# Start-up loads put into their order of use, and two small matrix products folded into one with two column groups

## The chip, the core and the metric

The kernel runs on one core of a Trainium2 chip. The metric is the device time of one execution in microseconds (us); less is better. Everything is float32.

## The reference

The reference adds two blocks to an input `x` of 2 sequences with 1024 tokens of 256 features. The first block (an attention layer with a "field", then a mixture of 64 small experts) is the only one that the change touches, and there only its attention. Cut to what matters:

```python
qkv = x @ Wqkv.T + bqkv                        # 16 heads of 16
attn = softmax(q @ k.T / sqrt(16))
coh = sigmoid(tanh([x, cs] @ Wc1.T + bc1) @ Wc2.T + bc2)   # cs: one row of 64 per sequence
mod = attn * coh;  mod = mod / (mod.sum(-1) + 1e-8)
fp = layernorm(relu(cs @ We1.T + be1) @ We2.T + be2)       # one row of 256 per sequence
pe = sin(pos / inv)                            # a table, 1024 x 256
fa = softmax(fp @ pe.T)                        # 2 x 1024: the field
mod = (1 - FI) * mod + FI * fa[:, None, None, :]
out = (mod @ v) @ Wout.T + bout
```

The field `fa` is small: for each of the 2 sequences one softmax over 1024 positions.

## The kernel before

The engines are TensorE (PE), VectorE (DVE), ScalarE (ACT), GpSimd (POOL) and SyncE (SP). A framework sets the semaphores, and also the order of instructions on each engine, from a schedule that it works out when the program is built. Inside a `manual_schedule` block PE, DVE and ACT keep the order in which the code is written; POOL and SP do not, they get what the framework's schedule finds ready.

**Loads.** At the start, ACT issues the load of `cols` (L107), then three parts of the attention weights `w_att`: the first halves of `wq` and `wk` and the whole of `wv` (L155 to L165). SP issues the two halves of `xT` for sequence 0 (L134, L135), then the second halves of `wq` and `wk`, and `wout`. POOL issues `w_cs`, `w_pro`, `rows`, `xT` for sequence 1 and the table `peT` (L468 to L474).

**The lead (L680 to L717).** The attention works on 8 units of 16 steps. Each step of `maxima(step, half)` (L304) makes 2 x 2 score products into a two-bank PSUM tile `pm`, and DVE reduces each tile to its row maxima (L320). Such tiles come from `wide` (L180), which turns through three of them in this part: one of pool `ps_3`, two of `ps_s`. A step makes two tiles, so the second tile of step m+1 needs the buffer that the first tile of step m held only after DVE has read it. All the rest takes single PSUM banks from `one` (L195), two buffers in turn.

Ahead of the lead stand the q and k projections of unit 0 (`project_part`, L280), `spread(0)` (L297; eight SP transfers that scatter the heads into `km` and `qm`), `from_state`, two `coherence_in` (L535: two products, then a tanh on ACT), and two `values` (L204: products into `pv`, then, as here `lead` is set, an ACT copy into `v`, L224, and a POOL add of the bias, L225).

The lead itself is 12 steps; after the two `maxima` of step m come the pieces of `fill[m]`:

```python
[field_in, coherence_in(0, 1, 0)],           # m = 0
[field_mean, coherence_in(0, 1, 1)],
[field_var, values(0, 1, 0)],
[values(0, 1, 1), spread(1)],                # then matrices()
[field_logits(0)],  [field_logits(1)],       # m = 4, 5
[coherence_in(1, 0, 0), field_weights],  [coherence_in(1, 0, 1), field_scale],
[coherence_in(1, 1, 0)],  [coherence_in(1, 1, 1), field_out],
[shift(0), rotation(mats)],  [coherence_out]
```

`matrices` (L492) is called after step 3 and makes, on POOL, two 256 x 256 matrices out of 32 blocks of 64 x 64 (L506). `field_logits(n)` (L628) multiplies `fpc` (128 x 2) with half n of `peT` into a bank of 2 rows x 512 columns, takes the row maxima and their negative on DVE, and the exp and its sum on ACT. `field_weights` (L647) combines the halves' maxima on DVE (`fall`), makes weights on ACT (`fw`), and sums on POOL. `field_scale` (L654) takes a reciprocal on DVE, scales `fw` on POOL and the two halves of `fe` on ACT. `field_out` (L660) turns `fe` by eight transposes on PE into `fac`.

**Behind the lead.** 128 steps follow (L770), each with score products, exps, the product with `v` (L365) and, while there are any, the `maxima` of twelve steps later. `between` (L732 to L765) hangs other pieces on some of them; L756 hangs `values(1, n, part)` for both parts on step 2 and 5 of unit 2. Then come the experts and the second block, which the change does not touch.

## Time and profile before

| | us |
|---|---|
| median of 3 runs | 1551.67 (1550.71 to 1555.02) |
| the profiled execution's own time | 1551.6 |
| its span, first to last instruction | 1549.8 |
| PE / DVE / ACT / POOL busy | 1528.1 / 891.1 / 881.5 / 529.3 |
| first matmul starts | 6.44 |
| first score product of the 128 steps (L347) starts | 63.38 |

The profiled execution is 0.07 us under the median, and 1.8 us of it lie outside the span. The table is read as follows: PE is busy for 99% of the span, and the other engines for 34% to 57%. All that the change touches lies in the first 63.4 us of the span, except for one piece in unit 2, at 184 us. Times given as places ("at 48.21") are us from the span's start. A line of the trace's timeline gives the start, the length, the engine and line, the operation with what it writes and reads, how many instructions are merged into it, and in brackets the idle time of the engine before it.

### The profile page before, as it was taken

To read this page: it belongs to the slowest core of one execution; us is meant where nothing else is said; L and a number is where in the kernel's file an instruction comes from. 1 tells how busy PE (TensorE), PEld (TensorE's weight loads), DVE (VectorE), ACT (ScalarE), POOL (GpSimd) and SP (SyncE) were. 2 spreads that over 40 slices of the span, in tenths; PEclk is the share of its full clock that TensorE was granted. 3 is DMA by queue.
4 is the path that set the end of the run, shared out by engine and by line. 5 is a ranking of instruction groups with operands and counts; after the bars stand their busy time and mean duration, and the time that the engine had idled before them with its cause. 6 is when DMAs were issued, how large, how long until landed. Compare 5 with 4: busy or idle time off the path is not lost.

```text
span 1549.8 us, 25956 instructions
## 1 busy us (share of the span) xinstructions
PE 1528.1 (99%) x10176; PEld 754.1 (49%) x10176; DVE 891.1 (57%) x1606; ACT 881.5 (57%) x1710; POOL 529.3 (34%) x863
## 2 busy tenths in 40 slices
PE   8999999999999999999999999999999999999999
PEld 4333343333333444444687667555555454545544
DVE  5868768776873222224455766656666565656531
ACT  2478768787887222224334554665757666666641
POOL 3333323333430100000102354555555555565411
PEclk9999999999999999999999999999999999999999
DMA  5100000010000526445843202000100001000001
GB/s 165 56 14 15 1 15 15 1 21 8 1 1 15 172 96 194 150 144 180 265 163 96 65 5 84 1 1 1 68 2 2 14 1 57 1 18 12 23 6 41
DMA packets 50441, 84.90 MB, mean 55 GB/s; under 512 B 4616, under 2 KB 25392, under 8 KB 50064
## 3 DMA queue, kind: packets, MB, share of 16 engines
q1 hardware_dynamic: 47776, 77.41, 16.0%
q0 software_dynamic: 1584, 5.29, 1.1%
q8 instruction: 80, 1.31, 0.3%
q10 hardware_dynamic: 960, 0.56, 0.1%
q14 instruction: 41, 0.34, 0.1%
HBM read 57.02 MB, written 22.02 MB: 51 GB/s over the span
## 4 chain that ended last, share of the span: by engine, by line
PE 93%; DVE 3%; ACT 2%; DMA 2%; POOL 0%; issue 0%; SPq 0%; ACTq 0%; POOLq 0%; DVEq 0%
PE pga L1451 9%; PE sc L347 9%; PE po L365 8%; PE pm L313 7%; PE lg L816 7%; PE sl L842 7%; PE pq L1161 7%; PE cmb L935 6%; PE py L1485 4%; PE pwo L1382 4%; PE po L1362 3%; PE pv L1231 3%; PE sc L1274 2%; PE pqk L283 2%; PE py L863 2%; PE pe L1246 2%
## 5 line engine op out<-in xcount | busy, mean ns | idle before, releaser
L320 DVE TENSOR_REDUCE mx<-pm 128x2 f32<-128x1024 f32 x256 | 301.5, 1219 | 108.1 <-PE pm L313 108.0
L355 ACT ACTIVATE e<-sc 128x512 f32<-128x512 f32 (+1 forms) x500 | 263.6, 614 | 67.8 <-PE pm L313 63.6
L347 PE MATMUL sc<-qs,km 32*128 32x512 f32 x1024 | 247.8, 617 | 0.7 <-ACT cg L565 0.7
L313 PE MATMUL pm<-km,qm 32*128 32x512 f32 x1024 | 242.9, 616 | 0.0
L383 POOL TENSOR_TENSOR ob<-ob,part 128x512 f32<-128x512 f32 x101 | 128.4, 1271 | 251.2 <-ACT part L382 251.2
L1451 PE MATMUL pga<-hc,w 128*128 128x512 f32 x320 | 143.0, 598 | 2.0 <-ACT eT L1349 0.8
L365 PE MATMUL po<-e,v 128*32 128x512 f32 x1024 | 136.9, 605 | 0.0
L347 PEld LDWEIGHTS sc<-qs,km 32*128 32x128 f32 x1024 | 91.7, 183 | 86.5 <-ACT e L355 65.2
L1328 POOL TENSOR_SCALAR eall<-eall,den 128x192 f32<-128x192 f32 (+1 forms) x128 | 113.8, 902 | 26.8 <-DVE den L1324 26.8
L935 PE MATMUL cmb<-xb,y 128*128 128x256 f32 x512 | 117.4, 383 | 0.0
L1161 PE MATMUL pq<-wqo,xa 128*128 128x512 f32 x256 | 116.1, 597 | 0.1
L816 PE MATMUL lg<-phi,xa 128*128 128x512 f32 x256 | 116.1, 596 | 0.0
L1312 ACT ACTIVATE eall<-eall,nmx 128x192 f32<-128x192 f32 (+1 forms) x256 | 111.1, 439 | 8.0 <-DVE nmx L1295 7.8
L842 PE MATMUL sl<-dsp,xb 128*128 128x512 f32 x256 | 114.9, 593 | 0.0
L1199 POOL TENSOR_TENSOR t<-raw,tabs 128x512 f32<-128x512 f32 x64 | 80.7, 1283 | 96.7 <-ACT raw L1191 96.6
L313 PEld LDWEIGHTS pm<-km,qm 32*128 32x128 f32 x1024 | 83.4, 184 | 49.2 <-DVE mx L320 34.9
L826 DVE TENSOR_TENSOR l<-lg,keep 128x512 f32<-128x512 f32 x32 | 22.1, 692 | 144.8 <-ACT keep L824 144.8
L935 PEld LDWEIGHTS cmb<-xb,y 128*128 128x128 f32 x512 | 95.5, 190 | 17.7 <-issue 4.4
L1451 PEld LDWEIGHTS pga<-hc,w 128*128 128x128 f32 x320 | 59.5, 190 | 73.0 <-issue 68.0
L1295 DVE CUSTOM_DVE_ANT_0 eall<-sc,mask,zn 128x192 f32<-128x192 f32 (+1 forms) x256 | 86.9, 405 | 7.0 <-PE sc L1274 7.0
L824 ACT COPY keep<-lg 128x512 f32<-128x512 f32 x32 | 18.7, 584 | 126.0 <-issue 101.0
L1191 ACT COPY raw<-pq 128x1024 f32<-128x1024 f32 x32 | 32.4, 1011 | 97.6 <-PE pq L1161 97.6
(228 smaller groups left out, 2366.3 us busy)
## 6 DMA issues: line engine op xcount, KB each, us to landing
lgd<-keep SPq DMA_DIRECT2D x64, 256.0 KB, 2.4
w<-in_ffn_W SPq DMA_DIRECT2D x16, 1024.0 KB, 7.1
ebig<-lgd SPq DMA_DIRECT2D x64, 256.0 KB, 3.6
wqo<-in_wqkv SPq DMA_DIRECT2D x2, 1536.0 KB, 7.7
w<-in_w SPq DMA_DIRECT2D x2, 1386.0 KB, 5.9
km<-hk SPq DMA_DIRECT2D x32, 64.0 KB, 2.3
qm<-hq SPq DMA_DIRECT2D x32, 64.0 KB, 2.3
phi<-in_phi SPq DMA_DIRECT2D x1, 2048.0 KB, 7.5
```

Source lines behind the costliest of these rows:

```text
L313: nc.tensor.matmul(pm[:, x, :], qm[u % 2][r, i * P : (i + 1) * P], km[u % 3][r, n * 512 : (n + 1) * 512], start=True, stop=True,)
L320: nc.vector.tensor_reduce(mxs[hu][:, i % 4, 2 * half : 2 * half + 2, n], pm, AX.X, ALU.max)
L347: nc.tensor.matmul(sc[:, x, :] if both else sc[x], km[u % 3][r, j * P : (j + 1) * P], qs[u % 2][r, n * 512 : (n + 1) * 512], start=True, s ...
L355: nc.scalar.activation(part, t, AF.Exp, scale=1.0 / HD0**0.5)
L365: nc.tensor.matmul(po[32 * hh : 32 * hh + 32, :], v[b][:, j, at : at + 32], es[s, hh // 2][:, hh % 2, :], start=True, stop=True,)
L383: nc.gpsimd.tensor_tensor(obs[u, n], obs[u, n], part, ALU.add)
L816: nc.tensor.matmul(lg[:, b, :], xa[:, k, b, 1 + m * P : 1 + (m + 1) * P], phi[:, k, n * 512 : (n + 1) * 512], start=(k == 0), stop=(k == 1),)
L842: nc.tensor.matmul(accs[n][b][:, c, :], xo_tm[:, b * 8 + m, c * P : (c + 1) * P], d[:, b, :], start=(m == 0), stop=(m == 7),)
L935: nc.tensor.matmul(acs[q][:, c, :], y[b][:, 4 * jj + j, c * P : (c + 1) * P], eT[:, j // 2, j % 2 * 256 : (j % 2 + 1) * 256], start=(jj == ...
L1161: nc.tensor.matmul(pq[:, x, :], shifted(xa, k, b, w * WIN, P), load["wqkv"][:, k, x * 512 : (x + 1) * 512], start=(k == 0), stop=(k == 1),)
L1328: engine.tensor_scalar(e[:, x, c, lo:KEYS], e[:, x, c, lo:KEYS], den[:, x, c : c + 1], None, ALU.mult)
L1451: nc.tensor.matmul(pt[:, x, :], load["w1"][:, k, lo : lo + P], hcs[f][:, k, :], start=(k == 0), stop=(k == 1))
```

## The change

1. The start-up loads. ACT now issues only `cols` and the first halves of `wq` and `wk` ahead. SP issues, behind the two halves of `xT`, the loads `w_cs`, `w_pro`, `wv` and `rows`. POOL issues no load at all. Behind the second tanh, ACT issues five more: `peT`, `xT` of sequence 1, the second halves of `wq` and `wk`, and `wout`.
2. `field_logits` is called once. `fpc`, filled up with zeros to 32 columns (`fpz`), is the weight of two column groups of the array, one for each half of `peT`; the results lie in partitions 0 to 31 and 32 to 63 of one bank. Maximum, negative and exp are then one instruction each, on 64 partitions.
3. To combine the halves, `field_weights` first copies the maxima and sums of the two groups side by side, with four copies on POOL; the DVE minimum (`fall`) now reads what those copies wrote. `field_scale` copies the weights back (two copies on POOL) and scales `fe` with one ACT instruction. `field_out` makes four transposes of 64 rows in place of eight of 2 rows.
4. The freed step of the lead: `field_weights`, `field_scale` and `field_out` come one step earlier (steps 5, 6 and 8), and step 9 takes `values(1, 0, 0)`, which leaves unit 2.

```diff
+    def load_att(engine, lo, n):
+        engine.dma_start(
+            w_att[:, :, lo : lo + n], a["w_att"][:, lo : lo + n].rearrange("(c p) n -> p c n", p=P)
+        )
     for engine, lo, n in (
         (nc.scalar, at0["wq"], P),
         (nc.scalar, at0["wk"], P),
-        (nc.scalar, at0["wv"], D),
-        (nc.sync, at0["wq"] + P, P),
-        (nc.sync, at0["wk"] + P, P),
-        (nc.sync, at0["wout"], D),
     ):
-        engine.dma_start(
...
+        load_att(engine, lo, n)
...
-        nc.gpsimd.dma_start(w_cs, a["w_cs"])
+        nc.sync.dma_start(w_cs, a["w_cs"])
...
-        nc.gpsimd.dma_start(w_pro, a["w_pro"].rearrange("(c p) n -> p c n", p=P))
+        nc.sync.dma_start(w_pro, a["w_pro"].rearrange("(c p) n -> p c n", p=P))
+        load_att(nc.sync, at0["wv"], D)
+        nc.sync.dma_start(rows, a["rows"].partition_broadcast(P))
         peT = pro.tile([P, 2, S], F32, name="peT")
-        nc.gpsimd.dma_start(rows, a["rows"].partition_broadcast(P))
-        load_x(nc.gpsimd, S, S)
-        nc.gpsimd.dma_start(peT, a["peT"].rearrange("(c p) n -> p c n", p=P))
...
                 nc.gpsimd.tensor_scalar(
-                    fpc[:, c, :], fpc[:, c, :], col("ln_g", c), col("ln_b", c), ALU.mult, ALU.add
+                    fpz[:, c, :B], fpc[:, c, :], col("ln_g", c), col("ln_b", c), ALU.mult, ALU.add
                 )
...
+        fpz = pro.tile([P, 2, 32], F32, name="fpz")
+        nc.gpsimd.memset(fpz, 0.0)
+        fnmx = pro.tile([64, 1], F32, name="fnmx")
...
-        def field_logits(n):
+        def field_logits():
-            fl = one("fl")[0:B]
+            fl = one("fl")
             for k in range(2):
-                nc.tensor.matmul(
-                    fl,
-                    fpc[:, k, :],
...
+                for n in range(2):
+                    nc.tensor.matmul(
+                        fl[32 * n : 32 * n + 32, :],
+                        fpz[:, k, :],
+                        peT[:, k, n * 512 : (n + 1) * 512],
+                        start=(k == 0),
+                        stop=(k == 1),
+                    )
...
+            nc.vector.tensor_reduce(fnmx, fl[0:64, :], AX.X, ALU.max)
+            nc.vector.tensor_scalar(fnmx, fnmx, -1.0, None, ALU.mult)
+            nc.scalar.activation(th["fe"], fl[0:64, :], AF.Exp, bias=fnmx, accum_out=fsum)
 
         def field_weights():
-            nc.vector.tensor_tensor(fall, fnmx[:, 0:1], fnmx[:, 1:2], ALU.min)
-            nc.scalar.activation(fw, fnmx, AF.Exp, bias=fall, scale=-1.0)
-            nc.gpsimd.tensor_tensor(fsum, fsum, fw, ALU.mult)
-            nc.gpsimd.tensor_tensor(fall, fsum[:, 0:1], fsum[:, 1:2], ALU.add)
+            for n in range(2):
+                nc.gpsimd.tensor_copy(fnm2[:, n : n + 1], fnmx[32 * n : 32 * n + B, :])
+                nc.gpsimd.tensor_copy(fsm2[:, n : n + 1], fsum[32 * n : 32 * n + B, :])
+            nc.vector.tensor_tensor(fall, fnm2[:, 0:1], fnm2[:, 1:2], ALU.min)
+            nc.scalar.activation(fw, fnm2, AF.Exp, bias=fall, scale=-1.0)
+            nc.gpsimd.tensor_tensor(fsm2, fsm2, fw, ALU.mult)
+            nc.gpsimd.tensor_tensor(fall, fsm2[:, 0:1], fsm2[:, 1:2], ALU.add)
 
         def field_scale():
             nc.vector.reciprocal(fall, fall)
             nc.gpsimd.tensor_scalar(fw, fw, fall, FI, ALU.mult, ALU.mult)
             for n in range(2):
-                nc.scalar.activation(th["fe"][:, n, :], th["fe"][:, n, :], AF.Identity, scale=fw[:, n : n + 1])
+                nc.gpsimd.tensor_copy(fws[32 * n : 32 * n + B, :], fw[:, n : n + 1])
+            nc.scalar.activation(th["fe"], th["fe"], AF.Identity, scale=fws)
 
         def field_out():
...
-            for i in range(S // P):
-                nc.tensor.transpose(pt[:, i, :], fe[:, i * P : (i + 1) * P], ident[0:B, 0:B])
...
+            for i in range(4):
+                nc.tensor.transpose(
+                    pt[:, i, :, :].rearrange("p n r -> p (n r)"), fe[:, i * P : (i + 1) * P], ident[0:64, 0:64]
+                )
...
             coherence_in(0, 0, 0)
             coherence_in(0, 0, 1)
+            nc.scalar.dma_start(peT, a["peT"].rearrange("(c p) n -> p c n", p=P))
+            load_x(nc.scalar, S, S)
+            for name, lo, n in (("wq", P, P), ("wk", P, P), ("wout", 0, D)):
+                load_att(nc.scalar, at0[name] + lo, n)
             values(0, 0, 0, True)
...
-                [lambda: field_logits(0)],
-                [lambda: field_logits(1)],
+                [field_logits],
                 [lambda: coherence_in(1, 0, 0), field_weights],
                 [lambda: coherence_in(1, 0, 1), field_scale],
                 [lambda: coherence_in(1, 1, 0)],
                 [lambda: coherence_in(1, 1, 1), field_out],
+                [lambda: values(1, 0, 0, True)],
                 [lambda: shift(0), lambda: rotation(mats)],
...
-        between[2, 2 + 3 * n] = [lambda n=n, part=part: values(1, n, part) for part in range(2)]
+        between[2, 2 + 3 * n] = [lambda n=n, part=part: values(1, n, part) for part in range(1 - n, 2)]
```

More of the change, by code (lines that the diff above doesn't have):

```diff
@@ L157, in tile_kernel @@
         (nc.scalar, at0["wk"], P),
-        (nc.scalar, at0["wv"], D),
-        (nc.sync, at0["wq"] + P, P),
-        (nc.sync, at0["wk"] + P, P),
-        (nc.sync, at0["wout"], D),
-    ):
-        engine.dma_start(
-            w_att[:, :, lo : lo + n], a["w_att"][:, lo : lo + n].rearrange("(c p) n -> p c n", p=P)
-        )
+    ):
+        load_att(engine, lo, n)
     mxt = [at1.tile([P, 4, 4, 32], F32, name=f"mxt{i}") for i in range(2)]
@@ L619, in field_var @@
                 nc.gpsimd.tensor_scalar(
-                    fpc[:, c, :], fpc[:, c, :], col("ln_g", c), col("ln_b", c), ALU.mult, ALU.add
+                    fpz[:, c, :B], fpc[:, c, :], col("ln_g", c), col("ln_b", c), ALU.mult, ALU.add
                 )
-        fnmx = pro.tile([B, 2], F32, name="fnmx")
-        fsum = pro.tile([B, 2], F32, name="fsum")
+        fpz = pro.tile([P, 2, 32], F32, name="fpz")
+        nc.gpsimd.memset(fpz, 0.0)
+        fnmx = pro.tile([64, 1], F32, name="fnmx")
@@ L625, in tile_kernel @@
+        fsum = pro.tile([64, 1], F32, name="fsum")
+        fws = pro.tile([64, 1], F32, name="fws")
+        nc.gpsimd.memset(fws, 0.0)
+        fnm2 = pro.tile([B, 2], F32, name="fnm2")
+        fsm2 = pro.tile([B, 2], F32, name="fsm2")
         fw = pro.tile([B, 2], F32, name="fw")
         fall = pro.tile([B, 1], F32, name="fall")
-        def field_logits(n):
-            fl = one("fl")[0:B]
+        def field_logits():
+            fl = one("fl")
             for k in range(2):
-                nc.tensor.matmul(
-                    fl,
-                    fpc[:, k, :],
-                    peT[:, k, n * 512 : (n + 1) * 512],
-                    start=(k == 0),
-                    stop=(k == 1),
-                )
-            if n == 0:
-                th["fe"] = at2.tile([P, 2, 512], F32, tag="e", name="fe", bufs=6)[0:B]
-            nc.vector.tensor_reduce(fnmx[:, n : n + 1], fl, AX.X, ALU.max)
-            nc.vector.tensor_scalar(fnmx[:, n : n + 1], fnmx[:, n : n + 1], -1.0, None, ALU.mult)
-            nc.scalar.activation(
-                th["fe"][:, n, :], fl, AF.Exp, bias=fnmx[:, n : n + 1], accum_out=fsum[:, n : n + 1]
-            )
@@ new lines, in field_logits @@
+            th["fe"] = at2.tile([P, 2, 512], F32, tag="e", name="fe", bufs=6)[0:64, 0, :]
+            nc.vector.tensor_reduce(fnmx, fl[0:64, :], AX.X, ALU.max)
+            nc.vector.tensor_scalar(fnmx, fnmx, -1.0, None, ALU.mult)
+            nc.scalar.activation(th["fe"], fl[0:64, :], AF.Exp, bias=fnmx, accum_out=fsum)
+        def field_weights():
+            for n in range(2):
[5 more added lines that the diff above has]
+            nc.gpsimd.tensor_tensor(fall, fsm2[:, 0:1], fsm2[:, 1:2], ALU.add)
@@ L657, in field_scale @@
             for n in range(2):
-                nc.scalar.activation(th["fe"][:, n, :], th["fe"][:, n, :], AF.Identity, scale=fw[:, n : n + 1])
+                nc.gpsimd.tensor_copy(fws[32 * n : 32 * n + B, :], fw[:, n : n + 1])
+            nc.scalar.activation(th["fe"], th["fe"], AF.Identity, scale=fws)
         def field_out():
-            fe = th.pop("fe").rearrange("p n t -> p (n t)")
-            pt = one("pfac")[:, : T // P].rearrange("p (i b) -> p i b", b=B)
-            for i in range(S // P):
-                nc.tensor.transpose(pt[:, i, :], fe[:, i * P : (i + 1) * P], ident[0:B, 0:B])
-            nc.vector.tensor_copy(fac.rearrange("p (b i) -> p i b", b=B), pt)
+            fe = th.pop("fe")
+            pt = one("pfac")[:, :256].rearrange("p (i n r) -> p i n r", i=4, n=2)
+            for i in range(4):
+                nc.tensor.transpose(
+                    pt[:, i, :, :].rearrange("p n r -> p (n r)"), fe[:, i * P : (i + 1) * P], ident[0:64, 0:64]
+                )
+            nc.vector.tensor_copy(fac.rearrange("p (b n i) -> p i n b", b=B, n=2), pt[:, :, :, :B])
         def rotation(mats):
```

## The prediction

> **What bounds the kernel now.** The page first: PE is busy for 99% of the span and makes 93% of the chain that ended last. So whatever PE must do more, or must wait for, is paid in full, and an engine beside it counts only where PE waits for it.

> ```profile
> PE 1528.1 (99%) x10176; PEld 754.1 (49%) x10176; DVE 891.1 (57%) x1606; ACT 881.5 (57%) x1710; POOL 529.3 (34%) x863
> ...
> PE 93%; DVE 3%; ACT 2%; DMA 2%; POOL 0%; issue 0%; SPq 0%; ACTq 0%; POOLq 0%; DVEq 0%
> ```

> Next the chain in order of time, over the stretch that the change rewrites (start, length, what):

> ```profile
> 39.26 1.81 PE fl L632 x4
> 41.07 1.07 PE pm L313 x8
> 42.14 1.81 PE fl L632 x4
> 43.95 1.07 PE pm L313 x8
> 45.02 1.91 PE pz L539 x4
> 46.93 1.07 PE pm L313 x8
> ...
> 60.82 1.90 PE pc L555 x16
> ```

> PE runs without a gap from 39.26 on: a step is 1.07 us of maxima products and some 1.9 of a filling piece. But the averages of the whole span hide what stands beside it. In the stages view PE is busy for 10.66 of the 10.66 us between 39.26 and 49.92, DVE for 10.35 and POOL for 9.81. So I read the timeline of POOL and of DVE there:

> ```profile
> 36.70 1.58 POOL L506 TENSOR_SCALAR m_rq<-ident,unit_rq 64x64 f32<-64x64 f32 x5
> 38.37 1.18 POOL L225 TENSOR_TENSOR v<-v,rows 128x512 f32<-128x512 f32 x1
> 39.65 3.42 POOL L506 TENSOR_SCALAR m_rq<-ident,unit_rq 64x64 f32<-64x64 f32 x11
> 43.15 4.97 POOL L506 TENSOR_SCALAR m_lq<-ident,unit_lq 64x64 f32<-64x64 f32 x16
> 48.21 1.18 POOL L225 TENSOR_TENSOR v<-v,rows 128x512 f32<-128x512 f32 x1
> 49.34 0.18 POOL L651 TENSOR_TENSOR fsum<-fsum,fw 2x2 f32<-2x2 f32 x1
> ...
> 42.34 2.33 DVE L320 TENSOR_REDUCE mx<-pm 128x2 f32<-128x1024 f32 x2
> ...
> 47.64 0.19 DVE L649 TENSOR_TENSOR fall<-fnmx 2x1 f32<-2x1 f32 x1
> ```

> POOL works without a pause from 36.7 to 49.4 on the 32 matrix blocks and two bias adds. The second add (of `values(0, 1, 1)`) is written ahead of the matrices in the code and its ACT copy ended at 38.8; yet it ran at 48.21, behind all 32 blocks. POOL's order is not the code's, is fixed when the program is built, and puts the blocks first. Today nobody suffers: the first field piece that needs POOL is the sum L651, and the DVE minimum at 47.64 reads only what DVE wrote.

> **The change, part by part.** All times are on the clock of this execution.

> *The field's products, removed work.* Two pieces of 1.81 become one of eight matmuls in two column groups. `pc` does the like: sixteen in four groups take 1.90, where one group of four takes 1.81. So the new piece is 1.81 to 1.90; I take 1.85 and save 3.62 - 1.85 = 1.8 us of PE, on the path.

> *The field's weights, an added wait.* The DVE minimum now waits for POOL copies, and these read what DVE writes after the products, at 42.4, later than the copy whose add came behind the blocks. So I expect the copies behind that add too: it starts at 48.21, L651 behind it at 49.34, L652 0.26 later. Two to four copies at 0.26 give 49.9 to 50.4; I take the third, which holds the second maximum if they go in the code's order: 50.1.
> What waits behind the minimum: DVE has read step 5's tiles at 44.67 (42.34 + 2.33) and keeps order, so the reductions of steps 6 and later stand still from 44.7 to 50.1. Who waits for these: PE goes on, products to 41.1, maxima of step 5 to 42.2, tanh product to 44.1, maxima of step 6 to 45.2, next tanh product to 47.1, and the first tile of step 7 (half of 1.07) to 47.6. Then all three wide buffers are full, and the second tile of step 7 needs the first reduction of step 6. That starts some 0.4 behind the minimum's start (47.64 to 48.04 now) and takes 1.21: 50.1 + 0.4 + 1.2 = 51.7. PE stands still from 47.6 to 51.7: **4.1 us**. From there on DVE stays ahead of what PE needs, by the same durations (step 8's first tile at 54.2 needs a reduction that ends at 52.9), so nothing is late next. Below: if POOL takes the copies between the blocks, a wait of under 1 us is hidden by the two spare tiles, so 0. Above: 4.4 with the fourth copy.

> *Scale and turn.* One ACT instruction of 0.67 replaces two (1.33), with two more POOL copies before it (0.5); `field_out` needs it three PE pieces later. Eight transposes took 0.52; four of full width take 0.59 in L331: +0.1.

> *The moved `values`.* In the lead a piece costs 1.92 (L211 at 36.27). In unit 2 two pieces cost 3.65 (L211 at 185.11), one 1.83: +0.1. Its ACT copy and POOL add replace one DVE add, beside PE.

> *The loads at the start.* The first matmul (6.44) waits for the first part of `wq`, which lands 5.1 after its issue at 1.19. The `xT` half beside it lands 4.6 after 0.73, at 5.3. POOL's loads begin at 6.05 and cannot have slowed it, and ahead of `wq` on ACT's and SP's queues nothing changes. I take 0; at best the start moves to `xT`'s landing, -1.0; at worst +0.3. [...] The loads now on SP are needed from 16.3 on; before, from POOL at 6.05 to 7.57, they landed within 5.2 to 5.7 us, so an issue before 5 is early enough. POOL's freed 3.5 us lie before 9.6, while its next work starts at 23.5: 0.

> *The five loads on ACT.* They stand between the second tanh (21.03) and the copy of `pv` (22.81, 24.48). An issue takes 0.45 to 0.49 when free: 2.4 in all, to 23.5; SP's first five took from 0.73 to 4.29, 3.56, to 24.6. The copies then end by 25.2 and 25.8; PE needs the first at 25.44, the second at 26.33: 0. The data are needed at 39.3 (`peT`) and 45.0 (`xT`), and 15 us cover landings of 7.9 and 10.3. SP's scatter transfers for unit 0 are issued by 21.0 and land 2.3 later, ahead of the bulk. But an issue can itself wait; see the second rival.

> **Sum:** -1.8 + 4.1 + 0.1 + 0.1 = +2.5; 1551.6 + 2.5 = **1554.1 us**, and as the profiled execution is 0.07 from the median, the same for the median.

> **The rivals.**

> *POOL takes the copies between the blocks* (13%). Then no stall: 1551.6 - 1.8 + 0.2 = 1550.0. For it: the add of `values(0, 1, 0)` did get in between, at 38.37. Against it: its input came 3 us earlier than the other add's, which did not.

> *ACT is held at its loads* (20%), the case that ends slower. In SP's wait list stands

> ```profile
> SPq L163 <- DMA cols<-in_cols: 0.4, 1, 0.4
> ```

> SP's last start-up load, the ninth from SP and ACT together, waited until the first of the nine had landed. If such a count of eight runs on, the last of ACT's five loads may fall on `peT`, the first of them, should four of SP's scatter transfers be counted in between. ACT would then stand still until `peT` lands. Issued at 21.1, it would land 5.3 later (the 512 KB halves from SP) to 7.5 (`phi`, 2048 KB), or 10.3 as `peT` does now. For 1024 KB I take the middle of the first two, 6.4: 27.5, then the issue 0.5, the copy 0.6 and a handover of 0.1: 28.7 in place of 25.44, +3.3, with 2.2 and 7.2 as ends. With the stall: 1557.4, slower by 0.37%. From a price of 2.2 on, a landing after 5.3, it passes the bound of 0.3%. Against it: the number in between must be exactly four.

> *The clock drops in the stall* (8%). PE's first sixteen products took 9.94 us where 0.43 each would be 6.9: weights were loaded every 0.86 us until about 12, then every 0.43. A stall of 4 us may bring that state back once: +3.0, 1557.1. Nothing in this trace shows a pause of such length. [...]

> *The start moves up by 1.0* (4%), with the stall: 1553.1.

> **How the numbers follow.** The forecast has 55%. The range takes in the first rival with the small errors, 1549.5, and the second to a little over its value, 1558.5; what is left out is a `peT` as slow as now, or both slow rivals at once. A change under 0.3% (4.65 us; about what a measurement of this kernel can tell from no change) is "same": the forecast, the first and the last rival, and half of the third, 0.76, from which I take 0.05 for a cause that I don't see on the faster side, as all savings together are only -2.6: 0.71. Slower: the second, and half of the third, whose price may be smaller than the 2.2 that it needs: 0.24.

> **What would show it.** In the profile after: `fl` once, eight matmuls in some 1.85 us; on DVE, idle time of about 5 us before the minimum `fall`, released by a POOL copy; on PE, an idle time of about 4 us before a `pm` product, released by DVE `mx`; POOL's blocks unbroken ahead of the copies; the first matmul still at 6.4; the copies of `pv` on ACT at most 1 us later than now; one `pv` piece in unit 2. The prediction is wrong if the copies stand between the blocks, if ACT's row shows a wait for a landing, or if the weight loads go to 0.33 us a second time.

## The result, and the profile after

The changed kernel takes 1560.89 us in the median of 6 runs (1560.05 to 1564.76), beside 1550.74 for 6 runs of the kernel before (1550.18 to 1555.02). The ratio is 1.0064, with a 95% interval of 1.0052 to 1.0075: it is slower by 10 us, four times what was forecast, and outside the range. The profiled execution took 1561.21 us with a span of 1559.4; that span is 9.6 longer than the one of before, and it is the one that is taken apart here.

First the two lines of the page that stood at the head of the prediction, now of the kernel after.

```profile
PE 1532.0 (98%) x10172; PEld 754.4 (48%) x10172; DVE 890.9 (57%) x1603; ACT 880.5 (56%) x1708; POOL 526.9 (34%) x867
...
PE 91%; DVE 3%; DMA 2%; ACT 2%; POOL 1%; issue 0%; ACTq 0%; SPq 0%; POOLq 0%
```

PE is busy 3.9 us longer with four instructions fewer, and the span grew by 9.6, so the loss is of two kinds: PE stood still for 5.7 us more (9.6 - 3.9), and was busy for 3.9 us longer, although work was taken out. The view of PE's waits (who waited for whom; sum, number of times, longest) has the first kind:

```profile
PE pqk L283 <- DMA w_att<-in_w_att: 6.3, 1, 6.3
PE pm L313 <- DVE mx L320: 3.0, 1, 3.0
...
PE sc L1287 <- DVE t L1192: 2.4, 1, 2.4
PE pfp L591 <- ACT v L224: 2.3, 1, 2.3
```

The first and the third row stand in the profile of before too (6.4 and 2.4). The second is the forecast stall. The fourth was not in the forecast's sum. The chain in order of time shows what lies behind both (start, length, what):

```profile
20.56 5.66 DMA peT<-in_peT
26.24 0.37 ACTq L157
...
26.71 0.59 ACT v L224
...
27.35 1.05 PE pfp L591 x8
28.41 3.52 PE pz L538 x4
...
51.80 1.17 POOL v L225
52.98 0.13 POOL fnm L653
...
53.16 0.18 POOL fnm L653
53.36 0.15 DVE fall L655
53.51 1.15 DVE mx L320
...
54.70 1.16 PE pm L313 x4
55.86 3.53 PE pz L538 x4
```

ACT's last load (L157, `wout`) was issued at 26.24, when the transfer of `peT` had landed, and the copy of `pv` came behind it. The tanh product `pz`, four matmuls, takes 3.5 us after each of the two waits, where it takes 1.98 elsewhere. The view by stages shows why (its columns are the stretch, its length, the busy time of PE, PE's weight loads, DVE, ACT and POOL, then PE's granted clock, the DMA share and GB/s):

```profile
28.35:31.76 3.41, 3.41 (x5) 0.98 (x4) 0.34 (x2) 0.00 (x0) 1.35 (x2) 0.50 0.78 180
31.77:51.73 19.96, 19.96 (x97) 8.35 (x96) 12.91 (x17) 6.91 (x11) 11.94 (x37) 1.00 0.08 15
55.66:59.07 3.41, 3.41 (x6) 1.17 (x4) 2.44 (x4) 0.72 (x1) 0.60 (x3) 0.50 0.00 0
898.75:902.16 3.41, 3.41 (x12) 2.67 (x9) 3.34 (x15) 3.21 (x16) 2.04 (x2) 0.50 0.19 74
```

In three stretches of 3.41 us each PE's clock was granted at half. Two lie behind the two new waits. The third lies in the second block, far from anything that was changed, behind the old wait of 2.4 us for DVE `t`, after which the execution of before shows no such stretch.

The field's stall is the forecast one. These are lines of the timelines of PE, POOL and DVE of the kernel after:

```profile
42.79 1.91 PE L638 MATMUL fl<-peT,fpz 128*32 128x512 f32 x8
...
50.60 1.13 PE L313 MATMUL pm<-km,qm 32*128 32x512 f32 x4
54.70 1.16 PE L313 MATMUL pm<-km,qm 32*128 32x512 f32 x4 [2.97 <-DVE mx L320]
...
46.74 4.97 POOL L505 TENSOR_SCALAR m_lq<-ident,unit_lq 64x64 f32<-64x64 f32 x16
51.80 1.17 POOL L225 TENSOR_TENSOR v<-v,rows 128x512 f32<-128x512 f32 x1
52.92 0.41 POOL L653 COPY fnm<-fnmx 2x1 f32<-2x1 f32 x2
...
53.36 0.15 DVE L655 TENSOR_TENSOR fall<-fnm 2x1 f32<-2x1 f32 x1 [5.08 <-POOL fnm L653]
```

One `fl` piece stands where there were two, the blocks are unbroken, the bias add comes behind them, the copies behind the add, and DVE idles for 5.08 us before the minimum. PE stands still for 2.97 us between the two tiles of step 7. Each tile alone takes as long (1.13 and 1.16) as the two of a step take together elsewhere (1.07, eight instructions): side by side they overlap, and the stall took that from them as well.

The terms, each from the starts of the same pieces in the two executions:

| term | us | from |
|---|---|---|
| start, up to the first `pm` | -0.47 | 24.37 to 23.90; full clock from 12.15, now 11.29 |
| wait of `pfp` for the copy of `pv` | +2.38 | `pm` to `pfp`: 1.07 to 3.45 |
| first half clock | +1.70 | `pz` to the next `pm`: 1.89 to 3.59 |
| field's products | -1.78 | 3.62 to 1.84 |
| stall at the minimum | +4.12 | last `pm` of the stall's step to its `pz`: 1.07 to 5.19 |
| second half clock | +1.62 | `pz` to the next `pm`: 1.91 to 3.53 |
| `values` into the lead, out of unit 2 | +0.14 | +1.86, -1.72 |
| third half clock | +1.63 | `sc` to `pe` at 898: 4.47 to 6.10 |
| sum | +9.34 | of 9.6 |

Of the 0.26 left over one part is known: in the first block's experts PE waits 0.5 for a load (`py` L876, for DMA `w`), which it does not do before. The smaller differences of the other sign were not traced.

### The profile page after: what moved, and what is told of

Its sections match the earlier page's. It is cut to its first block, busy times and chain, and to the rows that moved or that the text cites. A ratio compares the mean times of both kernels' runs of the same rounds, so it can differ in the third digit from the quotient of the medians.

```text
span 1559.4 us, 25950 instructions
## 1 busy us (share of the span) xinstructions
PE 1532.0 (98%) x10172; PEld 754.4 (48%) x10172; DVE 890.9 (57%) x1603; ACT 880.5 (56%) x1708; POOL 526.9 (34%) x867
## 3 DMA queue, kind: packets, MB, share of 16 engines
q10 hardware_dynamic: 2048, 2.91, 0.6%
## 4 chain that ended last, share of the span: by engine, by line
PE 91%; DVE 3%; DMA 2%; ACT 2%; POOL 1%; issue 0%; ACTq 0%; SPq 0%; POOLq 0%
PE pga L1464 9%; PE sc L347 9%; PE po L365 8%; PE lg L829 7%; PE pm L313 7%; PE sl L855 7%; PE cmb L948 7%; PE pq L1174 6%; PE py L1498 4%; PE pwo L1395 4%; PE po L1375 3%; PE pv L1244 3%; PE sc L1287 2%; PE pqk L283 2%; PE py L876 2%; PE pe L1259 2%
## 5 line engine op out<-in xcount | busy, mean ns | idle before, releaser
L320 DVE TENSOR_REDUCE mx<-pm 128x2 f32<-128x1024 f32 x256 | 301.5, 1219 | 112.7 <-PE pm L313 112.6
L313 PE MATMUL pm<-km,qm 32*128 32x512 f32 x1024 | 243.9, 616 | 3.0 <-DVE mx L320 3.0
L313 PEld LDWEIGHTS pm<-km,qm 32*128 32x128 f32 x1024 | 83.5, 183 | 53.9 <-DVE mx L320 36.5
```

The source lines that it names most:

```text
L313: nc.tensor.matmul(pm[:, x, :], qm[u % 2][r, i * P : (i + 1) * P], km[u % 3][r, n * 512 : (n + 1) * 512], start=True, stop=True,)
L320: nc.vector.tensor_reduce(mxs[hu][:, i % 4, 2 * half : 2 * half + 2, n], pm, AX.X, ALU.max)
```

## The experiments

The theory from here: three mechanisms add up that the prediction had set against each other. ACT is held at its loads until `peT` lands; DVE is held at the minimum behind POOL's blocks; and each pause of PE that this makes costs 1.6 to 1.7 more, since the clock drops. The rivals: one half of the change alone makes the loss; the bulk transfers themselves (0.78 of all DMA time in the first slow stretch) slow PE or its supply; the half clock comes from a time or a place and not from the pause.

### Each half alone

Two kernels: in the first the loads are those of before and the field is changed; in the second the loads are changed and the field is that of before (two `field_logits`, the old steps). So each is one part of the diff above, and no code is new.

> The field and the order of the lead as in the changed kernel, the loads as before. Theory A (three separate losses: ACT held at its loads until peT lands, DVE held at its minimum until POOL ends the matrix blocks, and a clock drop behind each of the two pauses of PE): the load loss and its drop are gone. The copies of pv are back at 22.8 and 24.5; DVE still idles about 5 us before its minimum and PE about 3 to 4 us before a maxima product; -1.8 + 4.1 + 0.1 = +2.5 against before, and +1.7 more if the clock drops behind the pause: 1553.2 to 1554.9. Theory B (all of the loss comes from where the loads stand, also the late POOL): DVE does not wait, and only the saved product is left: 1549.0.

> The loads as in the changed kernel, the field and the order of the lead as before. Theory A: ACT issues its fifth load only when peT has landed, at about 26.2; PE pauses about 2.3 us before the product pfp and the clock drops once behind it: +2.4 + 1.7 - 0.4 = +3.7 against before, 1554.4; DVE nowhere waits 5 us. Theory B (all of the loss comes from the loads): the whole +10, 1560.9. Theory C (all of it comes from the field): 1550.3 to 1550.7.

The field alone: 1557.47 us (1555.15 to 1560.04), ratio 1.0034 (1.0021 to 1.0046). The loads alone: 1555.79 (1554.6 to 1558.97), 1.0028 (1.0017 to 1.0039). Beside 1551.4 for before on the same chip these are +6.1 and +4.4; their sum of 10.5 is about what the whole change costs (10.2). Both medians lie above what the three mechanisms gave (1554.9 at most, and 1554.4). The excess goes with the clock: of the field alone, the two runs with a mean granted clock of 0.999, one of them the profiled one with a single half stretch in the middle of the program, took 1555.15 and 1555.24, and the four with 0.996 to 0.998 took 1556.68 to 1560.04. PE's timeline of the field alone, then of the loads alone:

```profile
46.63 1.13 PE L317 MATMUL pm<-km,qm 32*128 32x512 f32 x4
50.74 1.13 PE L317 MATMUL pm<-km,qm 32*128 32x512 f32 x4 [2.99 <-DVE mx L324]
51.80 3.26 PE L543 MATMUL pz<-xT,w_pro 128*128 128x512 f32 x4
```

```profile
27.77 1.06 PE L591 MATMUL pfp<-hid,w_pro 128*128 128x2 f32 x8 [2.55 <-ACT v L224]
28.69 3.65 PE L538 MATMUL pz<-xT,w_pro 128*128 128x512 f32 x4
```

Each half brings its own wait and its own slow stretch behind it. So neither half makes the loss alone, and as far as these medians tell the losses add.

### Four loads on ACT

`wout`, the load at which ACT stood, goes back to SP's queue at the start:

```diff
         nc.sync.dma_start(rows, a["rows"].partition_broadcast(P))
+        load_att(nc.sync, at0["wout"], D)
...
-            for name, lo, n in (("wq", P, P), ("wk", P, P), ("wout", 0, D)):
+            for name, lo, n in (("wq", P, P), ("wk", P, P)):
                 load_att(nc.scalar, at0[name] + lo, n)
```

> The changed kernel, but wout is loaded by SP at the start, behind rows, so that ACT has four loads behind the second tanh, none of which comes eight loads behind another that is still under way. Theory A: ACT's loads are all issued by about 23.5, the copies of pv end by 25.2, PE does not pause before pfp and the first clock drop is gone: 2.4 + 1.7 less than the changed kernel, 1556.8; the pause before the maxima product of step 7 stays at 4 us. Rival D (the bulk loads hurt by their traffic, as the scatter transfers and PE's operands come late): PE still waits about 2 us between 24 and 28, and the time stays at 1560 or above.

It took 1566.45 us (1565.86 to 1568.0), ratio 1.0095 (1.0078 to 1.0112): slower than the kernel after, where 4.1 us less were expected. By its time alone it fits the rival of the bulk traffic (1560 or above); the traces decide. Three timelines of it, of ACT, SP's queue and PE, and a row of the waits of SP's queue:

```profile
23.18 0.59 ACT L224 COPY v<-pv 128x512 f32<-128x512 f32 x1 [1.69 <-PE pv L211]
...
18.21 8.13 SPq L302 DMA_DIRECT2D qm<-hq  x4
...
30.30 2.07 PE L313 MATMUL pm<-km,qm 32*128 32x512 f32 x2 [5.03 <-DMA qm<-hq]
...
SPq L302 <- DMA peT<-in_peT: 5.8, 1, 5.8
```

ACT is free: the copy comes at 23.18. But SP's four `qm` transfers of unit 0, which take 2.4 us elsewhere, take 8.13. The last of them was issued only at 25.83, after a wait of 5.8 for `peT`. So it has the place that `wout` had in the kernel after: the eighth behind `peT`, with loads on ACT and scatter transfers on SP counted together. The trace confirms it: each DMA instruction in it names the semaphore (a counter that instructions can wait for) that its landing counts up, and `peT` and this `qm` have the same one (106), as `peT` and `wout` have in the kernel after (105). PE needs that `qm` for the second tile of step 0 and stands still for 5.03 us, and the clock is at half for 10.24 us (28.83 to 39.07). Not all of the 5.03 is the late issue: this `qm` also took 4.43 us to land, where such transfers take 2.3 in the median, and why it did is not shown. To take one load away did not end the wait; the wait went to the next transfer in the count.

### Two loads on ACT

Only `peT` and `xT` of sequence 1 stay behind the second tanh; the three parts of `w_att` go to POOL's queue at the start, which was POOL's place for loads before.

```diff
         nc.sync.dma_start(rows, a["rows"].partition_broadcast(P))
+        for name, lo, n in (("wq", P, P), ("wk", P, P), ("wout", 0, D)):
+            load_att(nc.gpsimd, at0[name] + lo, n)
...
-            for name, lo, n in (("wq", P, P), ("wk", P, P), ("wout", 0, D)):
-                load_att(nc.scalar, at0[name] + lo, n)
```

> The changed kernel, but only peT and xT of sequence 1 are issued by ACT behind the second tanh; the three weight loads go to POOL's queue at the start, which does not share the count of eight. Theory A (a load or transfer issued by ACT or SP waits until the one eight before it, in the order that the program was built in, has landed): nothing that unit 0 needs stands eight behind peT or xT, so neither ACT nor SP's transfers for unit 0 wait, PE has no pause of over 1 us before 40, no drop there: 2.4 + 1.7 less than the changed kernel, 1556.8, with the pause of 4 at step 7. Rival D (the bulk's traffic delays the transfers of unit 0): PE still pauses at 24 to 28, as 2 MB still move there.

1556.32 us (1555.93 to 1558.06), ratio 1.0035 (1.0023 to 1.0047); before, on the same chip, 1550.92. Timelines of ACT, SP's queue and PE:

```profile
21.77 0.59 ACT L224 COPY v<-pv 128x512 f32<-128x512 f32 x1 [1.09 <-PE pv L211]
...
19.92 7.50 SPq L302 DMA_DIRECT2D km<-hk  x4
...
24.41 1.05 PE L593 MATMUL pfp<-hid,w_pro 128*128 128x2 f32 x8
25.32 1.96 PE L540 MATMUL pz<-xT,w_pro 128*128 128x512 f32 x4
```

The wait for `peT` is still there: four `km` transfers take 7.50, and the second of them, on the semaphore of `peT`, was issued at 25.65, with `peT` landed at 25.63. But these are the transfers of unit 1, which nobody needs so early. ACT copies as it did before, and PE has neither the pause nor the slow `pz`. The loads' part of the loss is gone, though `peT` and `xT`, 2 of the 2.5 MB, still move at the same time; the rival of the bulk transfers falls. What is left (+5.4) is the field's stall, with a pause at 47.10 to 50.12, its half clock behind it, and the third half clock at 894.19.

### PE kept busy in its pauses

The kernel after, but two products are made several times, into the same tile with the same values: those of one tile of step 0 five times in all, and of one tile of step 7 six times. Nothing is left out; PE has more to do.

```diff
+    MORE = {(0, 1): 4, (7, 0): 5}
...
+        for o, w, m in again * (1 + MORE.get((step, half), 0)):
+            nc.tensor.matmul(o, w, m, start=True, stop=True)
```

> The changed kernel with work added that changes nothing in the output: the two products of the tile ahead of each pause of PE (second tile of step 0, first tile of step 7) are repeated four and five times into the same tile, some 2.1 and 2.7 us of products in the shade of the pauses of 2.3 and 3.0. Theory A (PE's clock is halved for 3.41 us behind a window of 3.41 us in which PE stood still for more than half): both drops in the lead are gone, and the kernel is faster for the added work, by 1.7 + 1.6: 1557.5; the waits for peT and for POOL are as long as before. Rival F (the drops come by chance, or from the transfers and not from PE's pause): the drops at 28 and 56 stay, 1560.9 or more.

1558.74 us (1556.58 to 1559.04), ratio 1.0045 (1.0029 to 1.006): faster than the kernel after by some 2 us, with 36 more matmul instructions. Timelines of ACT, DVE and PE, and its row of the stage view:

```profile
26.79 1.07 ACT L224 COPY v<-pv 128x512 f32<-128x512 f32 x2 [5.39 <-DMA peT<-in_peT]
...
52.95 0.15 DVE L654 TENSOR_TENSOR fall<-fnm 2x1 f32<-2x1 f32 x1 [5.15 <-POOL fnm L652]
...
24.06 4.57 PE L318 MATMUL pm<-km,qm 32*128 32x512 f32 x24
28.56 1.05 PE L590 MATMUL pfp<-hid,w_pro 128*128 128x2 f32 x8
29.48 1.96 PE L537 MATMUL pz<-xT,w_pro 128*128 128x512 f32 x4
```

```profile
28.35:31.76 3.41, 3.41 (x18) 1.88 (x20) 1.48 (x3) 0.28 (x1) 1.43 (x2) 1.00 0.74 181
```

ACT waits about as long for `peT` and DVE for POOL as they do after, and the DMA share is about the same (0.74 for 0.78). Only PE does not rest, and `pz` takes 1.96 at a granted clock of 1.00. So the half clock comes from PE's pause. The repeats ended 1.2 us later than the data came (`pfp` at 28.56; it was at 27.35), which is why the first score product of the 128 steps comes at 70.84, 1.9 and not 3.3 earlier than after.

### The field's pieces later

The stall at the minimum should go if the minimum is asked for when POOL is through with its blocks. The kernel after, with `field_weights`, `field_scale` and `field_out` on steps 7, 8 and 9 of the lead in place of 5, 6 and 8:

```diff
-                [lambda: coherence_in(1, 0, 0), field_weights],
-                [lambda: coherence_in(1, 0, 1), field_scale],
-                [lambda: coherence_in(1, 1, 0)],
-                [lambda: coherence_in(1, 1, 1), field_out],
-                [lambda: values(1, 0, 0, True)],
+                [lambda: coherence_in(1, 0, 0)],
+                [lambda: coherence_in(1, 0, 1)],
+                [lambda: coherence_in(1, 1, 0), field_weights],
+                [lambda: coherence_in(1, 1, 1), field_scale],
+                [lambda: values(1, 0, 0, True), field_out],
```

> The changed kernel, but the weights, the scaling and the turn of the field come two, two and one lead steps later (steps 7, 8 and 9), when POOL has ended the matrix blocks. Theory A: DVE waits under 1 us before its minimum, PE does not pause before step 7's product, the second clock drop is gone: 4.1 + 1.6 less than the changed kernel, 1555.2; the pause at the loads and its drop stay. Rival E (the loss in the field is in the two column groups or in the 64-row operations themselves): the time stays within 1 us of the changed kernel's 1560.9.

1556.3 us (1554.67 to 1557.88), ratio 1.0027 (1.0015 to 1.0039). PE has no pause at the field any more, and what is left is the wait of `pfp` (2.46, until 26.90) with 6.83 us of half clock behind it, and two more such stretches far behind the change (at 894.10 and 1460.71). The rival that blames the two column groups falls.

### Both mended, and the loads put back

Two loads on ACT together with the later field ("mended"); and the later field with the loads of before.

> The two loads of the run above, and the field's weights, scaling and turn on steps 7, 8 and 9. Theory A: no pause of PE over 1 us in the lead, no clock drop there, so what is left of the change is the saved product: 1.7 below before, 1549.6, or 1549.1 if the start is earlier by 0.4 as in the changed kernel's profile. A rival that the new order of the loads costs something by itself gives 1551 or more.

> The loads as before, and the field in two column groups with its weights, scaling and turn on steps 7, 8 and 9. Theory A: DVE waits under 1 us at its minimum, PE has no pause in the lead: 1.7 below before, 1549.6; equal to the run with two loads on ACT within 0.6. If the order of the loads is worth something by itself, this one is slower than that one.

Mended: 1550.85 us (1549.66 to 1552.73, 11 runs), ratio 1.0000 (0.9991 to 1.0008). Loads of before: 1550.98 (1550.03 to 1554.18, 11 runs), 1.0000 (0.9991 to 1.0008). In neither does PE pause for over 1 us in the lead. The whole loss is gone with the two waits, and no worth of the new order of the loads shows (0.13 us). But the 1.8 us of the field's products, which both still save, do not show in the time either: both are over 1 us above the 1549.6 expected. All 22 of these runs have a mean granted clock of 0.998 or 0.999; of the 22 runs of before on the same chip 15 have 1.000, and these take 1549.98 to 1551.35. PE's timeline of the mended kernel in the second block:

```profile
884.54 0.88 PE L1287 MATMUL sc<-kT,qT 64*64 64x192 f32 x16
887.88 0.88 PE L1287 MATMUL sc<-kT,qT 64*64 64x192 f32 x16 [2.45 <-DVE t L1192]
888.69 5.41 PE L948 MATMUL cmb<-xb,y 128*128 128x256 f32 x16
```

The pause of 2.45 us stands in every one of these kernels. Here the clock drops behind it (888.85 to 892.26 at 0.50), and `cmb` takes 5.41 where it takes 3.73 without a drop. If that is where the 1.8 went, work for PE in that pause must bring them back.

### The pause in the second block filled

The same edit on three kernels: the first score piece of step 1 of the second block is made three times in all, into the same tile with the same values, while PE would have waited anyway.

```diff
+            again = range(3 if (i, hg) == (1, 0) else 1)
-            for c in range(2):
+            for c in [c for _ in again for c in range(2)]:
```

> The mended kernel (three loads on POOL, field pieces on lead steps 7, 8, 9) with one edit far behind the change: in the second block, the first score piece of step 1 (0.88 us on PE) is made three times into the same tile with the same values, so that 1.76 of the 2.45 us in which PE waits there (885.43 to 887.88) are filled; DVE reads that tile only at 887.74. If the 1.8 us that the mended kernel saved are given back by the drop of the clock at 888.85, which follows the pause: the remaining pause is about 0.7 us, no weight loads at half the rate from 888 to 892, granted clock 1.000, span 1549.1 - 1.7 = 1547.4, time about 1549.1 in the median, and the interval below 1. If the drop comes from something else (a time since the start, a load on the chip): the drop stays and the time is 1550.9, as the pause that is filled was idle anyway. If the added products delay the next ones: up to +0.3 over that.

> The kernel with the loads of before and the later field, with the same edit as the mended and filled kernel: the first score piece of step 1 of the second block made three times. It lost its saving at the drop at 887.36 behind the pause of 2.45 us (884.92 to 887.37). If the pause is the cause: no drop there, clock 1.000, about 1551.0 - 1.7 = 1549.3, the same as the mended and filled kernel within 0.4, so that the new order of the loads is worth nothing in itself. If the order of the loads is worth something that other losses hid, the two differ by more than 0.5.

> Control: the kernel before with the same edit alone (the first score piece of step 1 of the second block made three times). Its profiled execution has the same pause of 2.44 us (887.71 to 890.15) but no drop behind it, since the pause lies across the bound of two windows. If so, nothing is to be had in such executions: 1550.6 to 1550.9 in the median, the same as before within 0.3, with fewer executions at a clock under 1.000. If filling the pause saves time by itself (the products behind start earlier), it would be about 1.7 faster, 1549.2, and the gain of the filled kernels would not be the clock's.

| kernel | us, 11 runs each | ratio to before (1551.71) | runs at clock 1.000 |
|---|---|---|---|
| mended and filled | 1549.39 (1548.33 to 1550.19) | 0.9984 (0.9975 to 0.9993) | 9 of 11 |
| loads of before, later field, filled | 1550.19 (1548.97 to 1551.45) | 0.9991 (0.9982 to 0.9999) | 7 of 11 |
| before, filled | 1551.21 (1550.5 to 1552.26) | 0.9996 (0.9986 to 1.0005) | 11 of 11 |

PE's timeline of the mended and filled kernel:

```profile
884.57 2.18 PE L1288 MATMUL sc<-kT,qT 64*64 64x192 f32 x48
887.90 0.88 PE L1288 MATMUL sc<-kT,qT 64*64 64x192 f32 x16 [1.15 <-DVE t L1192]
888.72 3.73 PE L948 MATMUL cmb<-xb,y 128*128 128x256 f32 x16
```

The second score piece starts at the same time (887.90), so the added products cost nothing and gain nothing by themselves; with the pause down to 1.15 us the clock stays, `cmb` takes 3.73, and the span is 1547.4, 1.7 less than the mended kernel's. The control shows that the edit by itself is worth little (-0.5, where at most 0.3 was expected, and the interval holds no change): all its runs are at 1.000, where 10 of the 27 of before are under it. Against this control the mended and filled kernel is 1.82 us faster, about the 1.8 of the field's products. The two kernels with the later field and the filled pause are the only versions here whose interval lies below 1, by 1.6 and 0.9 parts in a thousand, the second by a hair. The two filled kernels differ by 0.8 in the median, more than the 0.5 named beforehand as the sign that the order of the loads is worth something. But the two profiled executions differ in a drop of the clock at 1454.2 that only the one with the old loads has, and 4 of its 11 runs are under 1.000 beside 2; so that this 0.8 is the loads' own worth is not shown.

## Why the prediction was wrong

**The field's products, -1.8: right** (-1.78; the piece takes 1.84 to the next start, and 1.85 was taken).

**The field's weights, +4.1: the wait is right, the size (+4.12) by luck.** The blocks were unbroken, the add came behind them, the copies behind the add, DVE idled 5.08 before `fall`, and PE waited for the first reduction of step 6 at the second tile of step 7. With the field alone the minimum came at 49.41; 50.1 was forecast. But PE stood still for 2.97 us and not for 4.1. The prediction gave each tile half of the 1.07 of a step; alone a tile takes 1.13 and 1.16, since the two of a step otherwise overlap. So the step took 1.13 + 2.97 + 1.16 where the forecast amounts to 0.53 + 4.1 + 0.53: the pause was forecast 1.1 too long and the two tiles 1.2 too short, and the errors cancel. That the field by itself cost 6.1 in the median goes with the clock, which in its profiled execution came down behind the stall (`pz` 3.26 for 1.98).

**Scale and turn, +0.1, and the moved `values`, +0.1: right** within 0.2. The four transposes took a little less than the eight (0.39 for 0.52 in the chain), not more.

**The start, 0: right.** The first matmul starts at 6.35 for 6.44. Of the 0.47 gained by 23.90, 0.09 is this; the rest goes with the clock, which reached full speed at 11.29 and not at 12.15; in the other profiled executions it did so anywhere from 10.04 to 11.85, with old loads and new.

**The five loads on ACT, 0: this is the step that failed.** The step priced the issues when free (2.4 in all, to 23.5). Four of them were: the fourth ended at 22.8. The fifth waited until 26.24 for `peT`, which took 5.66 us. That is the second rival by its mechanism, and its price was not far off: 3.3 was taken, with 2.2 and 7.2 as ends, and it measured 2.4. What was wrong is its chance, 20%. It was held to need "exactly four" transfers in between, one number of several. Four it was: by the semaphores in the trace, three loads and four scatter transfers lie between `peT` and `wout`. But the runs with four and with two loads show that the question was put wrongly: in all three kernels `peT`, 5.0 to 5.7 us under way, held the eighth transfer counted behind it, on ACT's queue or on SP's. The eighth was ACT's `wout` (PE +2.4), SP's last `qm` of unit 0 (PE stood 5.0) or SP's second `km` of unit 1 (PE 0). To be safe from it the eighth had to be one that nobody needs soon, and most of those near the loads are needed soon.

**The clock, left out of the sum, 8%: the second failure.** "Nothing in this trace shows a pause of such length" was true, and the half clock came behind both pauses, 1.70 and 1.62 (the rival's price was 3.0). That the price might be smaller than 2.2, by which half of this rival's chance was counted as "same", no run had shown; the runs showed these 1.70 and 1.62. It came a third time at 898, 1.63, where no step of the prediction looked at all. Together that is 4.95, more than half of the excess over the forecast. The rival's pause was the forecast's own stall, so all that was open was whether such a pause brings the clock down, and 8% was too little for that.

**How the numbers followed: the rivals were treated as exclusive.** The range left out "both slow rivals at once". They were not rivals of the stall or of each other; each adds to it. The forecast with the prices of both, 1554.1 + 3.3 + 3.0 = 1560.4, lies within 0.5 of the median of after, but that is luck: the loads cost 2.4 and not 3.3, and the clock 4.95 in three drops and not 3.0 in one.

## What to carry to other kernels

Before a bulk load is put ahead of small transfers, count the transfers that follow on all the queues that share the count: here the eighth waited for the bulk to land, and who waited for that eighth decided whether it cost PE nothing (two loads), 2.4 us (the change) or 5.0 (four loads). Where TensorE is the bound, price the clock with a new pause: all 14 pauses between products here that had 1.74 us or more within one window of 3.413 (the table below) had the half clock behind them, and in the kernel after it cost 1.62 to 1.70 us, lasting one window each time (3.3 with the later field, where it lasted two: 7.18 from `pfp` to `pfm`, for 3.88 before). Look at the old pauses elsewhere too: in the kernel after, the one that ends at 898, far from the change, has a drop behind it that cost 1.63 us and that the execution of before does not show. Causes that lie in different places are added, not set against each other.

## What the runs showed of the hardware

| kernel | the pause's largest part in one window (us) | half clock behind it |
|---|---|---|
| four loads | 3.41 | yes |
| loads alone; field later; after; two loads | 2.50; 2.46; 2.31, 2.45, 2.44; 2.43, 2.45 | yes, each |
| mended; PE kept busy; later field with old loads (second block) | 2.44; 2.45; 2.44 | yes, each |
| field later (second block) | 2.14 | yes |
| mended; before; after; two loads; before filled (behind the last product of the program) | 2.00; 1.95; 1.84; 1.70; 1.57 | no, only one window later |
| field alone; four loads (second pause) | 1.79; 1.74 | yes |
| before; field alone, four loads (second block) | 1.66; 1.63, 1.62 | no |
| field later; old loads filled (a third place, between 1450 and 1465) | 1.48; 1.48 | yes |
| after; loads alone; two loads; mended; before; before filled (the same place) | 1.47 to 1.48 | no |
| loads alone (second block) | 1.44 | no |
| the other kernels (the same place, and behind the last product); the three filled kernels (second block) | 1.35 or less; 1.15 or less | no |

From 2.14 on all twelve bring it down, and up to 1.44 none does. Between them both occur: of the pauses between products those of 1.74 and 1.79 do, but behind the last product parts up to 2.00 do not. So the length of the pause alone is not the whole rule, and what else counts stays open. The third drop agrees with the grid: the pause of 2.44 us in the second block lies across a bound of two windows in the execution of before (0.78 and 1.66), which shows no drop, and within one window in the execution after, which shows one. Full speed began anywhere from 10.04 to 12.15 in the profiled executions, and 7 of the 22 runs of before beside the mended kernel have a mean granted clock under 1.000; that one kernel's pause falls on either side from run to run, and that this is part of the spread of its times, is the author's estimate from these numbers. Nor was a whole window idle in most cases: all but one of the drops marked "yes" in the table stand behind a window with 1.48 to 2.50 us of idle time.

**SP's and ACT's loads share a count of eight.** In these traces a transfer issued by one of them waited until the one eight places ahead had landed: in the kernel before SP's last start-up load, the ninth of the two, waited 0.4 us for `cols`, the first; in the kernel after `wout` was issued at 26.24, with `peT` landed at 26.22. The wait moves from ACT to SP with four loads and with two, and the semaphores in the traces show the count: SP's and ACT's transfers take eight of them in turn (in the kernel after 100, 102 to 106, 108 and 109), and ACT's five loads behind the second tanh each wait for the last landing on their own. `peT` shares its semaphore with `wout` in the kernel after, with the last `qm` of unit 0 with four loads, and with the second `km` of unit 1 with two. Loads on POOL's queue are not counted: they have semaphores of their own (111 to 115 in the kernel before, 111 to 113 with two loads).
